# Four mixture-of-experts layers: the next pass's routing woven into the last combine of the pass before, and the first destination mask kept in program order

## The chip, the cores and the metric

The kernel runs on one core of a Trainium2 chip. That core has five engines, each with its own queue of instructions: TensorE (PE, matrix products; its weight loads are shown as PEld), VectorE (DVE), ScalarE (ACT), GpSimd (POOL) and SyncE (SP), which here only issues transfers. Engines wait for one another through semaphores. The metric is the device time of one execution in microseconds (us), the median of several runs.

## What is computed

The input `x` holds T = 2048 tokens of D = 256 numbers. Four layers follow each other; each adds half of a feed-forward block, then an attention block, then half of the same feed-forward block again, each on the layer-normed `x`:

```python
x = x + 0.5 * ffn(layernorm(x))
x = x + attn(layernorm(x))
x = x + 0.5 * ffn(layernorm(x))
```

So the feed-forward block of layer n runs twice, and the second run of layer n is followed at once by the first run of layer n + 1. The feed-forward block is a mixture of experts (layer 1; the others differ in sizes and details):

```python
logits = xf @ gate_w.T
probs = softmax(logits)
topk_p, topk_i = top_k(probs, 2)
h = silu(xf @ w1[e]) * (xf @ w2[e])      # for each expert e
y = sum over the token's two experts of topk_p * (h @ w3[e])
sh = silu(xf @ sw1.T) * (xf @ sw2.T) @ sw3.T   # the shared expert, every token
return y + sh
```

Layer 0 (f0) has 7 experts of width 128, weights by a sigmoid, and a limit on how many tokens an expert keeps. Layers 1 and 3 (f1, f3) have 8 experts of width 176; in f3 the shared expert is 704 wide and gated by a sigmoid for each token. Layer 2 (f2) has 16 experts of width 128 and a Gelu without a product. All numbers are fp32.

## The kernel before

**Blocks and passes.** The tokens are held on chip as 16 tiles of 128 rows, in NB = 4 blocks of 512 tokens (four tiles each). One run of a feed-forward block is one `Sparse` object, a pass. The text calls them 0a, 0b, 1a, 1b, 2a, 2b, 3a, 3b: layer, and first or second run. The object of the b pass is `now`, that of the next layer's a pass is `following`.

**Steps of a pass**, in the order of the program (`body`):

- `norm(j)` normalizes block j: on VectorE statistics (L290, L291), the variance (L269) and a reciprocal (L271) around a square root on ScalarE (L270), then four row tiles on ScalarE (L297). Each row tile also carries the token's number.
- `columns(j)` turns the rows with eight PE transposes (L280), copies them to `hT` on VectorE and ScalarE (L281), multiplies by the router (L788), copies (L796), turns back (L798) and copies the logits to `lg` (L800).
- `choose(j)` finds the best two experts of each token in a chain of small VectorE operations (L836 to L848).
- `place(j)` counts with two PE products how many tokens go to each expert before each token (L883, L884), works out the slot of each token on VectorE (L888 to L903), and lets POOL scatter the rows to their slots in memory (`sent`): eight indirect transfers a block (L913). Then `weigh(j)` makes the softmax weights of the block: two subtractions, two Exp on ScalarE (L865, L867), a sum, a reciprocal and two products.
- `tables()` works out on VectorE which expert each tile of 128 slots belongs to and where its rows lie (`r_which`, `r_row`). SP reads `r_row` before it fetches.
- The routed experts go tile by tile in a pipeline (`experts`): `fetch` loads four tiles of rows into `got` by SP (L1007) and makes on VectorE a mask and the destination rows (`d_m`, `d_has`, `d_dest`, L1011 to L1017, five small operations); `turn` transposes (L1027) and copies to `hs` (L1029); `first`, `flip` and `second` are the expert's products (L1042, L1060, L1072); POOL scatters the result back (L913).
- `combine(j)` loads the two results of each token (`mine`, by SP) and adds them to `x` with their weights: eight VectorE operations a block (L1099).

**The shared expert** (`glu_pieces`) is cut into pieces that `beside(amount)` puts between the other steps: for each chunk PE makes the products (`up`, L330), ScalarE the activation (L337; L334 in f2), VectorE the product `mid` (L338; none in f2); then four times PE multiplies by the second matrix (`y`, L345) and VectorE adds into `x` (L349). `ahead` says how many blocks of it may run before the routed experts (3 in f1, otherwise 2); `beside(1000)` puts what remains of them behind `tables()`; the other blocks come with the combines.

**What sets the order.** PE's order is the program's (a manual schedule). VectorE's order is the program's only around the combines, so for `combine` and what follows each of them; elsewhere a scheduler orders it, and an instruction marked with `keep_in_program_order` keeps its place. Whatever the order, an engine works through its queue in that order: an instruction whose input is missing holds up all behind it.

**At the end of a b pass** the loop over blocks is

```python
for j in range(NB):
    beside(7 if j else 10)
    while j >= self.ahead and self.shares <= j:
        beside(1)
    self.combine(j)
    after(j)
```

with `after` the next pass's `norm`. The next pass's `body(every, ...)` then arranges all four blocks: columns, choose, place. In a b pass blocks 0 and 1 are arranged inside the attention, and only blocks 2 and 3 in `body`.

Of the kernel before, what the change touches and what calls it, by code (L numbers as in the profile page):

```python
# [183 lines left out]
class Net:  # L184
# [80 lines left out]

    def rstd(self, out, var, scale, eps):

        nc = self.nc
        nc.vector.tensor_scalar(out, var, scale, eps, ALU.mult, ALU.add)  # L269
        nc.scalar.activation(out, out, AF.Sqrt)  # L270
        nc.vector.reciprocal(out, out)  # L271

# [11 lines left out]
    def norm_block(self, j, tiles):  # L284

        nc = self.nc
        mv = self.small.tile([P, 4, 2], F32, tag="mv", name="mv")
        for q in range(4):
            st = self.small.tile([P, 6], F32, tag="st", name="st")
            nc.vector.bn_stats(st, self.x[4 * j + q])  # L290
            nc.vector.bn_aggr(mv[:, q, :], st)  # L291
        rs = self.small.tile([P, 4], F32, tag="rs", name="rs")
        self.rstd(rs, mv[:, :, 1], 1.0, 1e-5)
        mr = self.small.tile([P, 4], F32, tag="mr", name="mr")
        nc.vector.scalar_tensor_tensor(mr, mv[:, :, 0], -1.0, rs, ALU.mult, ALU.mult)
        for q in range(4):
            nc.scalar.activation(  # L297
                tiles[q], self.x[4 * j + q], AF.Identity, bias=mr[:, q : q + 1], scale=rs[:, q : q + 1]
            )
# [18 lines left out]

    def glu_pieces(self, pool, hT, j, up, dn, func, scale, gate=None):


        nc = self.nc
        nch, nm = up.shape[1], up.shape[2]
        mids = []
        for c in range(nch):
            ps = []
            for m in range(nm):
                t = self.bank("up", 4)
                for k in range(KD2):
                    nc.tensor.matmul(t, lhsT=up[:, c, m, k, :], rhs=hT[:, k, :], start=(k == 0), stop=(k == KD2 - 1))  # L330
                ps.append(t)
            mid = pool.tile([P, 512], F32, tag="mid", name="mid", bufs=nch + 4)
            if nm == 1:
                nc.scalar.activation(mid, ps[0], func)  # L334
            else:
                act = pool.tile([P, 512], F32, tag="act", name="act", bufs=3)
                nc.scalar.activation(act, ps[0], func)  # L337
                nc.vector.tensor_tensor(mid, act, ps[1], ALU.mult)  # L338
            mids.append(mid)
            yield KD2 * nm  # L340
        for q in range(4):
            i = 4 * j + q
            y = self.bank("y")
            for c in range(nch):
                nc.tensor.matmul(  # L345
                    y[:, :D], lhsT=mids[c][:, q * P : (q + 1) * P], rhs=dn[:, c, :], start=(c == 0), stop=(c == nch - 1)
                )
            by = scale if gate is None else gate[:, i : i + 1]
            nc.vector.scalar_tensor_tensor(self.x[i], y[:, :D], by, self.x[i], ALU.mult, ALU.add)  # L349
            yield nch / 2  # L350

# [379 lines left out]
class Sparse:  # L731
# [7 lines left out]

    def __init__(self, net, w, n, e, width, func, gated=False, ahead=1, capacity=False, fill=None):  # L740


        self.net, self.nc, self.tc = net, net.nc, net.tc
        self.w, self.n, self.e, self.width, self.func = w, n, e, width, func
        self.gated, self.ahead, self.fill = gated, ahead, fill
        self.const = {k: net.c[k] for k in ("ones", "below", "ids", "later4")}
# [11 lines left out]
        self.normed = set()  # L758
        self.got, self.dest, self.hs, self.mids, self.midT, self.reg = {}, {}, {}, {}, {}, {}


# [8 lines left out]
    def norm(self, j):  # L770
        if j in self.normed:
            return
        self.normed.add(j)
        self.net.norm_block(j, self.net.row_tiles(j))
        ins = self.nc.vector.tensor_scalar(
# [4 lines left out]
    def columns(self, j):  # L780
        nc, net, e = self.nc, self.net, self.e
        hT = self.hT[j] = net.hT[j] = net.to_columns(net.row_tiles(j), j)
# [3 lines left out]
        for k in range(KD2):  # L786
            for q in range(4):
# [5 lines left out]
                    stop=(k == KD2 - 1),  # L793
                )
        rows = net.routes.tile([P, P], F32, tag="r_lgT", name="r_lgT", bufs=2)
        nc.vector.tensor_copy(rows, ps[:, :P])  # L796
        ps = net.bank("t")
        nc.tensor.transpose(ps[:, :P], rows, net.c["ident"])  # L798
        lg = self.lg[:, 4 * j : 4 * j + 4, :]
        nc.vector.tensor_copy(lg, ps[:, :P].rearrange("p (q e) -> p q e", e=32)[:, :, : self.lg.shape[2]])  # L800
# [52 lines left out]

    def weigh(self, j):

        nc, e = self.nc, self.e
        if self.capacity:
            nc.vector.tensor_scalar(
                self.wt[:, :, 4 * j : 4 * j + 4], self.wt[:, :, 4 * j : 4 * j + 4], 0.5, None, ALU.mult
            )  # L860
            return
        first, second = self.wt[:, 0, 4 * j : 4 * j + 4], self.wt[:, 1, 4 * j : 4 * j + 4]
        p = self.small([P, 4, e], "r_p")
        nc.vector.tensor_tensor(p, self.lg[:, 4 * j : 4 * j + 4, :e], first.unsqueeze(2).to_broadcast([P, 4, e]), ALU.subtract)
        nc.scalar.activation(p, p, AF.Exp)  # L865
        nc.vector.tensor_tensor(second, second, first, ALU.subtract)
        nc.scalar.activation(second, second, AF.Exp)  # L867
        m = self.small([P, 4], "r_m")
        nc.vector.tensor_reduce(m, p, AX.X, ALU.add)
# [4 lines left out]
    def place(self, j):  # L874
# [30 lines left out]
        for q in range(4):  # L905
            for k in range(2):
                self.scatter("to", self.net.sent, slot[:, k, q : q + 1], self.rows[:, 4 * j + q, :])
        self.weigh(j)

# [89 lines left out]
    def fetch(self, s):  # L999
# [10 lines left out]
        m = self.tile([P, self.G], "d_m", bufs=3)[:, :q]  # L1010
        nc.vector.tensor_tensor(m, t[:, :q, D + 1], self.less[:, s : s + q], ALU.not_equal)  # L1011
        nc.vector.scalar_tensor_tensor(m, m, float(T), number, ALU.mult, ALU.add)
# [90 lines left out]
    def arrange(self, blocks, beside):  # L1103

        for j in blocks[:2]:
            self.norm(j)
        if len(blocks) < NB:
            beside(7)
# [7 lines left out]

    def body(self, blocks, after):


        nc, net, n, e, cap = self.nc, self.net, self.n, self.e, self.capacity  # L1120
        with (
# [9 lines left out]
            self.edn = net.load(keep, f"{n}_edn", parts=2)  # L1131
            gate = None
            if self.gated:
                gate = keep.tile([P, NT], F32, tag="sgate", name="sgate")

            def shared(js):
                for j in js:
                    if self.gated:
                        by = slice(4 * j, 4 * j + 4)
                        nc.scalar.activation(gate[:, by], self.lg[:, by, e], AF.Sigmoid)  # L1140
                        nc.vector.tensor_scalar(gate[:, by], gate[:, by], 0.5, None, ALU.mult)
                    yield from net.glu_pieces(
                        mids, self.hT[j], j, self.w[f"{n}_up"], self.w[f"{n}_dn"], self.func, 0.5, gate
                    )
                    self.shares = j + 1

            self.shares = 0

            def other():
                if self.fill:  # L1150
                    for _ in range(22):
                        self.fill.step()
                        yield 1
                yield from shared(range(self.ahead))

            work = other()

            def beside(amount):
                while amount > 0:
# [3 lines left out]
                    amount -= done  # L1163

            with net.tc.manual_schedule(engines={mybir.EngineType.PE}):
                self.arrange(blocks, beside)
                if self.number == 1:
                    self.pad()
                self.tables()
                beside(1000)  # L1170
                if cap:
# [3 lines left out]
                if self.fill:  # L1175
                    self.fill.rest()
                work = shared(range(self.ahead, NB))
                if cap:
                    nc.vector.tensor_tensor(self.wt, self.wt, cap.kept, ALU.mult)
                with net.tc.manual_schedule(engines={mybir.EngineType.DVE}):  # L1180
                    for j in range(NB):
                        beside(7 if j else 10)
                        while j >= self.ahead and self.shares <= j:
                            beside(1)
                        self.combine(j)
                        after(j)

# [634 lines left out]
def kernel(ctx: ExitStack, tc: tile.TileContext, io, out: bass.AP):  # L1822
# [3 lines left out]

    def experts(n, w, fill=None):
        if n == 0:
            return Sparse(net, w, "f0", 7, P, AF.Silu, ahead=2, capacity=True, fill=fill)
        if n == 2:  # L1830
            return Sparse(net, w, "f2", 16, P, AF.Gelu, ahead=2)
        return Sparse(net, w, f"f{n}", 8, 176, AF.Silu, gated=(n == 3), ahead=(3 if n == 1 else 2))

# [23 lines left out]
    for n in range(4):  # L1857
        if n:
            w = layers[n].w
            with stage() as net.psum:  # L1860
                following.body(every, normed)
            now = experts(n, w)
            with stage() as net.psum:
                left = (attn1, attn2, attn3)[n - 1](net, w, now)
        if n < 3:
            layers[n + 1] = Layer(net, n + 1).load()
            following = experts(n + 1, layers[n + 1].w)
        with stage() as net.psum:
            now.body(left, following.norm if n < 3 else store)
        layers[n].stack.close()  # L1870
# [18 lines left out]
```

## Time and profile before

| | us |
|---|---|
| median of 3 runs (3324.53 to 3328.82) | 3327.32 |
| the profiled execution | 3326.3 |
| its span, from the first to the last instruction | 3324.5 |

| engine | busy us | share of the span |
|---|---|---|
| PE | 2972.3 | 89% |
| PEld (beside PE) | 2040.4 | 61% |
| DVE | 1764.3 | 53% |
| POOL | 1342.6 | 40% |
| ACT | 1260.2 | 38% |

The mean clock that the throttle granted PE is 0.936 of full speed. In the trace a pass begins some us before the one ahead of it has ended. The times from the span's start that the text needs: combine(0) of 0b at 1350.5 and the first turn of 1a at 1446.2 (transition 0b-1a); combine(0) of 1b at 2012.0 and the first turn of 2a at 2092.4 (1b-2a); combine(0) of 2b at 2691 and the first turn of 3a at 2796.6 (2b-3a). The first turn of 1b is at 1902.0, that of 3b at 3157.3. A "turn" is L1027.

How to read it: busy time is a sum over the span. What a change is worth is read from the stage it touches: from who waited last there. Some views show single instructions with the idle time of their engine before them and, behind an arrow, the instruction whose end released them.

### The profile page before, as it was taken

What the parts mean: (1) busy time and instruction counts of PE and PEld (TensorE: products, weight loads), DVE (VectorE), ACT (ScalarE), POOL (GpSimd) and SP (SyncE); (2) the same over time, 40 slices, a digit from 0 to 9 for tenths busy, and PEclk for the clock granted to TensorE, in tenths of its full rate; (3) what the DMA queues carried; (4) which work ended last, traced back from release to release, by engine and by line L of the source; (5) the groups of instructions that cost most, each with busy time, mean ns of one, the idle gap of its engine ahead of it and who ended that gap; (6) DMA issues with size and microseconds to landing.
All of it is one profiled execution on the core that took longest, in us unless ns stands there. A gap on an engine that the chain in (4) does not pass through costs nothing. (4 is left out here: it accounts for less than half of the span.)

```text
span 3324.5 us, 44449 instructions
## 1 busy us (share of the span) xinstructions
PE 2972.3 (89%) x14098; PEld 2040.4 (61%) x14098; DVE 1764.3 (53%) x4824; ACT 1260.2 (38%) x2755; POOL 1342.6 (40%) x1616
## 2 busy tenths in 40 slices
PE   5769999999999967798899896789998779988899
PEld 3647777777777746466455574644554546655575
DVE  4646666666666676634743336345775453344433
ACT  3333222333223333433623244434775452335331
POOL 3436666766667534333211133531334433302230
PEclk9889999999999988899999998887998889997999
DMA  6333333323211023433000324441112542312132
GB/s 214 120 101 91 93 97 98 102 83 89 86 43 42 29 100 118 149 100 128 9 13 26 114 90 151 153 117 45 32 33 78 175 161 89 99 35 68 58 92 90
DMA packets 203340, 300.01 MB, mean 90 GB/s; under 512 B 30200, under 2 KB 156792, under 8 KB 201752
## 3 DMA queue, kind: packets, MB, share of 16 engines
q1 hardware_dynamic: 174840, 219.67, 22.6%
q0 software_dynamic: 28272, 77.51, 6.6%
q8 instruction: 118, 1.93, 0.2%
q14 instruction: 110, 0.90, 0.1%
HBM read 178.78 MB, written 118.04 MB: 89 GB/s over the span
## 5 line engine op out<-in xcount | busy, mean ns | idle before, releaser
L913 POOL DMA_INDIRECT back<-res,d_dest x326 | 312.6, 959 | 532.6 <-ACT res L1076 436.2
L913 POOL DMA_INDIRECT sent<-rows,r_slot x256 | 247.8, 968 | 505.6 <-issue 371.7
L1042 PE MATMUL up<-f_eup,hs 128*128 x1304 | 356.4, 397 | 9.9 <-issue 8.6
L330 PE MATMUL up<-hT,f_up 128*128 128x512 f32 x704 | 327.2, 620 | 6.2 <-DVE mid L338 4.6
L1072 PE MATMUL y<-f_edn,midT 88*128 (+1 forms) x964 | 263.9, 383 | 0.0
L345 PE MATMUL y<-f_dn,mid 128*128 128x256 f32 x768 | 201.3, 416 | 52.3 <-DVE x L349 25.4
L1042 PEld LDWEIGHTS up<-f_eup,hs 128*128 128x128 f32 x1304 | 214.1, 196 | 54.2 <-issue 14.8
L330 PEld LDWEIGHTS up<-hT,f_up 128*128 128x128 f32 x704 | 140.2, 201 | 169.9 <-issue 158.0
L1029 DVE COPY hs<-t 128x256 f32<-128x256 f32 x326 | 137.6, 423 | 184.1 <-PE t L1027 183.8
L665 PE MATMUL up<-vo,hT 128*128 128x256 f32 x1024 | 226.7, 379 | 0.0
L545 ACT COPY mid<-up 128x256 f32<-128x256 f32 x192 | 71.4, 372 | 393.0 <-PE up L541 390.0
L546 DVE TENSOR_TENSOR o<-up,mid 128x512 f32<-128x512 f32 x192 | 132.5, 691 | 163.4 <-ACT mid L545 163.2
L665 PEld LDWEIGHTS up<-vo,hT 128*128 128x128 f32 x1024 | 194.3, 190 | 40.0 <-issue 15.0
L525 POOL TENSOR_TENSOR ddq<-d0q,d2q 128x256 f32<-128x256 f32 x128 | 218.4, 1737 | 0.0
L345 PEld LDWEIGHTS y<-f_dn,mid 128*128 128x128 f32 x768 | 155.1, 208 | 102.3 <-DVE mid L338 33.0
L1027 PE MATMUL t<-c_ident,got 128*128 128x128 f32 x652 | 132.8, 287 | 77.2 <-DMA got<-sent 65.5
L338 DVE TENSOR_TENSOR mid<-act,up 128x512 f32<-128x512 f32 x112 | 76.5, 686 | 215.4 <-PE up L330 191.2
L1048 ACT ACTIVATE eact<-up 128x176 f32<-128x176 f32 (+1 forms) x232 | 70.6, 304 | 313.6 <-PE up L1042 300.7
L1435 POOL TENSOR_SCALAR_AFFINE_SELECT p<-p 128x512 f32<-128x512 f32 (+1 forms) x192 | 92.4, 482 | 230.6 <-ACT p L1418 146.3
L1072 PEld LDWEIGHTS y<-f_edn,midT 88*128 88x128 f32 (+1 forms) x964 | 158.8, 192 | 15.6 <-ACT midT L1062 1.3
L1378 DVE TENSOR_REDUCE mx<-a 128x2 f32<-128x512 f32 (+1 forms) x192 | 123.9, 688 | 79.9 <-PE a L1377 79.6
L337 ACT ACTIVATE act<-up 128x512 f32<-128x512 f32 x112 | 66.7, 596 | 241.6 <-PE up L330 240.7
(358 smaller groups left out, 6374.6 us busy)
## 6 DMA issues: line engine op xcount, KB each, us to landing
got<-sent SPq DMA_DIRECT2D x326, 129.0 KB
sent<-rows SPq DMA_DIRECT2D x64, 516.0 KB
mine<-back SPq DMA_DIRECT2D x64, 512.0 KB
dbc<-dd SPq DMA_DIRECT2D x64, 384.0 KB
f_eup<-in_f_eup_dram SPq DMA_DIRECT2D x16, 704.0 KB
f_eup<-in_f_eup_dram SPq DMA_DIRECT2D x14, 512.0 KB
f_edn<-in_f_edn_dram SPq DMA_DIRECT2D x8, 704.0 KB
back<-res,d_dest POOLq DMA_INDIRECT x326, 2.4
```

The source lines that it names most:

```text
L330: nc.tensor.matmul(t, lhsT=up[:, c, m, k, :], rhs=hT[:, k, :], start=(k == 0), stop=(k == KD2 - 1))
L345: nc.tensor.matmul(y[:, :D], lhsT=mids[c][:, q * P : (q + 1) * P], rhs=dn[:, c, :], start=(c == 0), stop=(c == nch - 1))
L525: nc.gpsimd.tensor_tensor(dd[:, 2 * f, u], shifted(d0[:, f])[u], d2[:, f], ALU.subtract)
L546: nc.vector.tensor_tensor(o[:, i], sides.rearrange("p (u n) -> p u n", u=2), t.unsqueeze(1).to_broadcast([P, 2, N]), ALU.add,)
L665: nc.tensor.matmul(ps[:, u * 256 : (u + 1) * 256], lhsT=hT[j][:, k, q * P : (q + 1) * P], rhs=vo.vo[:, h, k, :], start=(k == 0), stop=(k = ...
L913: ins = self.nc.gpsimd.indirect_dma_start(out=out, out_offset=bass.IndirectOffsetOnAxis(ap=index, axis=0), in_=in_, in_offset=None).ins
L1027: nc.tensor.transpose(ps[:, k * P : (k + 1) * P], got[:, k * P : (k + 1) * P], self.net.c["ident"])
L1029: nc.vector.tensor_copy(t, ps[:, : KD2 * P].rearrange("p (k t) -> p k t", k=KD2))
L1042: nc.tensor.matmul(ps[:, :ncol], lhsT=hs[:, k, :], rhs=up[:, bass.ds(x, 1), k, :], start=(k == 0), stop=(k == KD2 - 1))
L1072: nc.tensor.matmul(y[:, :D], lhsT=midT[:, c, :], rhs=dn[:, bass.ds(x, 1), c, :], start=(c == 0), stop=(c == parts - 1))
L1378: nc.vector.tensor_reduce(out, by, AX.X, ALU.min, negate=True)
L1435: self.nc.gpsimd.affine_select(out=e, in_=e, pattern=[[0, n], [1, P]], compare_op=ALU.is_ge, fill=0.0, base=0, channel_multiplier=-1)
```

## The change

- `glu_pieces` is split: `glu_steps` yields, for each piece, `products` (PE and ScalarE) and `rest` (VectorE) as two calls, so that VectorE's part can be issued later than PE's.
- `norm` is split into `moments` (statistics, variance, square root) and `norm_rows` (the rest). `columns` is split into `columns_only` (to the router's product), `turn_logits` and `logits`.
- `weigh` runs once in a pass, for all 16 tiles, after `tables()`, and not once for each block at the end of `place`.
- The first `d_m` of each pass keeps its place in the program, so on VectorE it stands behind the pieces of the shared expert.
- The end of a b pass is `onward(then, issue, settle)`: between `combine(j)` and `norm(j)` of the pass stand columns, choose and place of the next pass's block j - 1, all in VectorE's written order, with pieces of the next pass's shared expert (`issue` calls products, `settle` the VectorE parts issued before). `early` says how many blocks of it may be used so (2 in f1 and f2, 1 in f3).
- So the next pass's `body` gets no blocks to arrange: it begins with `tables()`. The first run of f2 has `ahead` 3 in place of 2. The shared expert's buffers grow with `bufs`.

In the counts per engine VectorE has 114 instructions fewer, ScalarE 61 fewer (25 of them loads of an activation table); PE, POOL and SP issue as many as before. The core of the diff:

```diff
+    def glu_steps(self, pool, hT, j, up, dn, func, scale, gate=None, bufs=None):
         nc = self.nc
         nch, nm = up.shape[1], up.shape[2]
-        mids = []
-        for c in range(nch):
+        mids, acts, sums = {}, {}, {}
+        def chunk(c):
             ps = []
             for m in range(nm):
                 t = self.bank("up", 4)
                 for k in range(KD2):
                     nc.tensor.matmul(t, lhsT=up[:, c, m, k, :], rhs=hT[:, k, :], start=(k == 0), stop=(k == KD2 - 1))
                 ps.append(t)
-            mid = pool.tile([P, 512], F32, tag="mid", name="mid", bufs=nch + 4)
+            mids[c] = pool.tile([P, 512], F32, tag="mid", name="mid", bufs=bufs or nch + 4)
             if nm == 1:
-                nc.scalar.activation(mid, ps[0], func)
+                nc.scalar.activation(mids[c], ps[0], func)
             else:
                 act = pool.tile([P, 512], F32, tag="act", name="act", bufs=3)
                 nc.scalar.activation(act, ps[0], func)
-                nc.vector.tensor_tensor(mid, act, ps[1], ALU.mult)
-            mids.append(mid)
-            yield KD2 * nm
-        for q in range(4):
-            i = 4 * j + q
-            y = self.bank("y")
+                acts[c] = act, ps[1]
+        def gated(c):
+            if nm == 2:
+                act, ps = acts.pop(c)
+                nc.vector.tensor_tensor(mids[c], act, ps, ALU.mult)
+        def down(q):
+            y = sums[q] = self.bank("y")
             for c in range(nch):
                 nc.tensor.matmul(
                     y[:, :D], lhsT=mids[c][:, q * P : (q + 1) * P], rhs=dn[:, c, :], start=(c == 0), stop=(c == nch - 1)
                 )
+        def into(q):
+            i = 4 * j + q
             by = scale if gate is None else gate[:, i : i + 1]
-            nc.vector.scalar_tensor_tensor(self.x[i], y[:, :D], by, self.x[i], ALU.mult, ALU.add)
-            yield nch / 2
+            nc.vector.scalar_tensor_tensor(self.x[i], sums.pop(q)[:, :D], by, self.x[i], ALU.mult, ALU.add)
+        for c in range(nch):
+            yield KD2 * nm, lambda c=c: chunk(c), lambda c=c: gated(c)
+        for q in range(4):
+            yield nch / 2, lambda q=q: down(q), lambda q=q: into(q)
...
-    def weigh(self, j):
+    def weigh(self):
         nc, e = self.nc, self.e
         if self.capacity:
-            nc.vector.tensor_scalar(
-                self.wt[:, :, 4 * j : 4 * j + 4], self.wt[:, :, 4 * j : 4 * j + 4], 0.5, None, ALU.mult
-            )
+            nc.vector.tensor_scalar(self.wt, self.wt, 0.5, None, ALU.mult)
             return
-        first, second = self.wt[:, 0, 4 * j : 4 * j + 4], self.wt[:, 1, 4 * j : 4 * j + 4]
-        p = self.small([P, 4, e], "r_p")
-        nc.vector.tensor_tensor(p, self.lg[:, 4 * j : 4 * j + 4, :e], first.unsqueeze(2).to_broadcast([P, 4, e]), ALU.subtract)
+        full = [P, NT, e]
+        first, second = self.wt[:, 0], self.wt[:, 1]
+        p = self.tile(full, "r_p", bufs=1)
+        nc.vector.tensor_tensor(p, self.lg[:, :, :e], first.unsqueeze(2).to_broadcast(full), ALU.subtract)
         nc.scalar.activation(p, p, AF.Exp)
         nc.vector.tensor_tensor(second, second, first, ALU.subtract)
         nc.scalar.activation(second, second, AF.Exp)
-        m = self.small([P, 4], "r_m")
+        m = self.tile([P, NT], "r_sum", bufs=1)
         nc.vector.tensor_reduce(m, p, AX.X, ALU.add)
         nc.vector.reciprocal(first, m)
         nc.vector.tensor_scalar(first, first, 0.5, None, ALU.mult)
...
-        self.weigh(j)
...
-        nc.vector.tensor_tensor(m, t[:, :q, D + 1], self.less[:, s : s + q], ALU.not_equal)
+        ins = nc.vector.tensor_tensor(m, t[:, :q, D + 1], self.less[:, s : s + q], ALU.not_equal)
+        if s == 0:
+            self.tc.keep_in_program_order(ins)
...
+    def onward(self, then, issue, settle):
+        for j in range(NB + 1):
+            p = j - 1
+            if j < NB:
+                if j:
+                    self.beside(7)
+                while j >= self.ahead and self.shares <= j:
+                    self.beside(1)
+                self.combine(j)
+            settle()
+            if p >= 0:
+                ps = then.columns_only(p)
+            if j < NB:
+                of = self.net.moments(j)
+            if p >= 0:
+                ps = then.turn_logits(ps)
+            if j < NB:
+                then.norm_rows(j, *of)
+            if p >= 0:
+                issue()
+                then.logits(p, ps)
+                then.choose(p)
+                then.place(p)
+                settle()
+                issue()
+    def body(self, blocks, after=None, then=None):
...
                 self.tables()
+                self.weigh()
                 beside(1000)
...
-                work = shared(range(self.ahead, NB))
+                work = self.shared(mids, range(self.ahead, NB), bufs)
                 if cap:
                     nc.vector.tensor_tensor(self.wt, self.wt, cap.kept, ALU.mult)
                 with net.tc.manual_schedule(engines={mybir.EngineType.DVE}):
-                    for j in range(NB):
-                        beside(7 if j else 10)
-                        while j >= self.ahead and self.shares <= j:
-                            beside(1)
-                        self.combine(j)
-                        after(j)
+                    if then:
+                        beside(10)
+                        nch = then.w[f"{then.n}_up"].shape[1]
+                        steps = enumerate(then.shared_steps(mids, range(then.early), bufs))
+                        late = []
+                        def settle():
+                            while late:
+                                late.pop(0)()
+                        def issue():
+                            for i, (_, products, rest) in steps:
+                                i %= nch + 4
+                                if i == nch:
+                                    settle()
+                                products()
+                                late.append(rest)
+                                if i < nch or (i - nch) % 2:
+                                    return True
+                        self.onward(then, issue, settle)
+                    else:
+                        for j in range(NB):
+                            beside(7 if j else 10)
+                            while j >= self.ahead and self.shares <= j:
+                                beside(1)
+                            self.combine(j)
+                            after(j)
+                if then:
+                    while issue():
+                        settle()
+                    settle()
...
-            return Sparse(net, w, "f2", 16, P, AF.Gelu, ahead=2)
-        return Sparse(net, w, f"f{n}", 8, 176, AF.Silu, gated=(n == 3), ahead=(3 if n == 1 else 2))
+            return Sparse(net, w, "f2", 16, P, AF.Gelu, ahead=3 if first else 2, early=2)
+        return Sparse(
+            net, w, f"f{n}", 8, 176, AF.Silu, gated=(n == 3), ahead=(3 if n == 1 else 2), early=(2 if n == 1 else 1)
+        )
 
...
-                following.body(every, normed)
+                following.body([], normed)
...
-            following = experts(n + 1, layers[n + 1].w)
+            following = experts(n + 1, layers[n + 1].w, first=True)
         with stage() as net.psum:
-            now.body(left, following.norm if n < 3 else store)
+            if n < 3:
+                now.body(left, then=following)
+            else:
+                now.body(left, store)
         layers[n].stack.close()
```

## The prediction

> **What bounds the kernel now.** I read the page first: PE is busy 89% of the span, so the time changes only where PE stands still or runs at half clock, at a stage whose end the next one needs. So I went to what PE waited for over the whole run (total us, times, longest us):
>
> ```profile
> PE t L1027 <- DMA got<-sent: 65.5, 5, 20.4
> PE y L345 <- DVE x L349: 25.4, 7, 5.4
> PE y L345 <- DVE mid L338: 23.2, 12, 7.1
> PE up L330 <- DVE mid L338: 4.6, 2, 4.0
> ```
>
> The first row is the start of the routed experts (L1027 turns the first gathered rows). The next three are the shared expert: PE waits for VectorE to multiply `mid` or to add into `x`. The longest of them, 7.1 and 4.0, are single events in the passes 1b and 3b. VectorE's timeline at the first (start, us, engine, what; in brackets the idle time before it and its releaser), then at the second:
>
> ```profile
> 1867.76 0.69 DVE L338 TENSOR_TENSOR mid<-act,up 128x512 f32<-128x512 f32 x1 [2.56 <-PE up L330]
> 1875.48 0.16 DVE L1011 TENSOR_TENSOR d_m<-got,r_less 128x4 f32<-128x4 f32 x1 [7.03 <-DMA got<-sent]
> ...
> 1878.32 0.69 DVE L338 TENSOR_TENSOR mid<-act,up 128x512 f32<-128x512 f32 x1
> ```
>
> ```profile
> 3129.05 0.16 DVE L1011 TENSOR_TENSOR d_m<-got,r_less 128x4 f32<-128x4 f32 x1 [8.90 <-DMA got<-sent]
> ...
> 3131.48 0.69 DVE L338 TENSOR_TENSOR mid<-act,up 128x512 f32<-128x512 f32 x1
> ```
>
> VectorE stands in order at `d_m`, whose gather has not landed, and a ready `mid` is queued behind it. PE then pays again at half clock. Stretches (length; busy PE, PEld, DVE, ACT, POOL; granted clock; DMA share; GB/s), the stalls of 1b and 3b first, then the transitions 0b-1a, 1b-2a, 2b-3a:
>
> ```profile
> 1871.00:1879.00 8.00, 0.95 (x5) 0.49 (x3) 1.91 (x10) 0.00 (x0) 0.00 (x0) 0.72 0.70 187
> 1879.00:1886.00 7.00, 6.94 (x19) 5.68 (x20) 2.10 (x11) 0.00 (x0) 0.00 (x0) 0.59 0.05 15
> 1886.00:1893.00 7.00, 7.00 (x18) 3.23 (x18) 1.15 (x3) 1.19 (x2) 0.00 (x0) 1.00 0.00 0
> ...
> 3132.00:3138.00 6.00, 5.77 (x8) 2.50 (x9) 2.85 (x12) 0.00 (x0) 0.00 (x0) 0.55 0.10 28
> ```
>
> ```profile
> 1364.00:1446.00 82.00, 63.76 (x252) 36.57 (x253) 45.73 (x219) 32.14 (x48) 30.69 (x32) 0.86 0.43 136
> ...
> 2030.00:2103.00 73.00, 37.78 (x176) 24.72 (x177) 44.97 (x209) 28.79 (x50) 32.99 (x33) 0.69 0.30 97
> ...
> 2720.00:2797.00 77.00, 67.44 (x263) 40.45 (x263) 36.88 (x166) 30.72 (x44) 30.91 (x32) 0.91 0.32 95
> ```
>
> Three transitions, three limits. In the first PE is idle 18 of 82 us, waiting for VectorE's chain. In the second PE has 38 us of work in 73, and the end is POOL's: 32 scatters of rows (L913) run from 2046.5 to 2088.6, one each 1.27 us. In the third PE is busy from 2745 to the first turn at 2796.6, though the gather landed at 2778.
>
> **The change, part by part.** Durations are this execution's. Its time is 3326.3 us (span 3324.5); the median of the runs is 3327.3, so I add 1.0 at the end.
>
> *The first d_m in program order.* It now stands behind the last add into `x` of the shared pieces, so what queues behind a late gather is only the first `hs` copies, which need the gather too. 1b: the 7.1 goes; what is late next is that `mid` itself, with its activation (0.60) and product (0.69), of which two y matmuls (0.4) cover some: 0.9 stays. Half clock at 0.59 over 7 us lost 2.9 us of full-clock work; a short wait may keep some, I take 2.5. After the stall PE is busy to the first turn at 1902, long after the gather, so all of it reaches the end: -8.7 (bounds -6.2, -9.1). 3b: 4.0 less 0.5, and 6 us at 0.55 lost 2.7, of which 2.5: -6.0 (-3.5 to -6.7). Against it, two or more groups of five small VectorE operations (0.2 apart) now come beside the first turns: +0.3 in each of five passes, +1.5 (0 to +4).
>
> *Transition 0b-1a.* Before, the four choices (router columns, choose, place) follow the four combines and share VectorE with Exp waits; place's matmuls come at 1376.4, 1393.4, 1404.8, 1416.2. After, combine(1) still follows the adds of block 3 (ends 1362.9), and one block's period on VectorE, in order, is: combine 8 x 0.396 = 3.17; `mid` 0.69; `hT` copy 0.69; statistics 4 x 0.53 = 2.1; variance to Sqrt's end, with its table load (1.283), 1.73; reciprocal and two small ones 0.4; logits 0.2; choose, 12 steps of 0.22, 2.5; place's matmuls and back 0.97; place 1.5; a second `mid` 0.69. Sum 14.8. Place(0) on PE: 1362.9 + 0.7 + 2.1 + 0.2 + 1.7 + 0.4 + 0.2 + 2.5 = 1370.7; two periods, then a last of some 10 without combine and norm: 1410. After it PE has the y of block 1 (6.2), block 2 (10.5 and 6.2) and perhaps one chunk (3.6), 26.5, so the first turn is at 1437 instead of 1446.2, about when the gather can land. The pieces between a block's logits and its place take 3.6 at full clock, under the chain's 4.8, but up to 7.2 at half clock: 2.4 more in each period puts it at 1442. Ends: -9 and, with place(3) 5 us late, +2. The former `d_m` stalls here (3.1 and 2.0) are in these. I take -5: PE has 11.7 us of work in 14.8 and should mostly keep its clock.
>
> *Transition 1b-2a.* Combine(1) waits as before for the late adds of block 3 (2024.6). Place(0): 2024.6 + 3.2 + 0.7 + 2.1 + 0.2 + 1.7 + 0.4 + 0.3 + 3.0 (64 columns, 0.25 a step) = 2036; scatters start at 2039.5, 7 earlier. But blocks then come each 14.2 and not each 10.9: 2053.7, with two adds 2068.8, and eight scatters take 10.1, so the last block's start at 2079 and end at 2089. POOL's gain at the front is lost to its gaps: 0 (-2 to +8). The tables, with the weights now ahead of them, are ready about 2088, just in time. A third block's shared expert moves into PE's idle 2072 to 2092. That shortens the end of 2a: there the add of block 3 between combine(0) and (1) held VectorE from 2180.03 to 2183.58 and PE had both left blocks; with one block I take -3.4 (0 to -7). Fewer half-clock us at the experts' start: -1 (0 to -2).
>
> *Transition 2b-3a.* Place(3) at about 2759 both ways; PE is the bound with the same 24 up and 24 y matmuls: 0 (-5 to +6). On SP's queue three loads of the next experts' weights stand ahead of the last `mine`, as they do in 1b-2a now; the gather of `mine` is early there: 0.
>
> *Weights once per pass.* 114 VectorE and 61 ScalarE instructions go, 25 of these table loads of 1.283. In the passes inside a layer PE's fill covers them (no wait of PE names Exp): -1 (0 to -3). SP's and POOL's instruction counts do not change.
>
> Sum: -8.7 - 6.0 + 1.5 - 5 + 0 - 3.4 - 1 + 0 - 1 = -23.6, from 3326.3 to 3302.7; with 1.0, 3303.7, say 3303.5.
>
> [...]
>
> **The rivals.** (1) *Slower: the interleaved loop runs at half clock.* PE's gaps in each block (waits for `hT`, `r_lgT`, `r_both`, up to 3.8 in the trace) keep the clock at 0.50, as it was from 2042 to 2050. Then both pieces of a block (3.6) take up to 7.2 and come ahead of place and of the next columns: period 14.8 + 2.4 + 3.6 = 20.8. 0b-1a: 1370.7 + 41.6 + 16 + 26.5 = 1454.8, +9. 1b-2a: place(3) 2094, scatters to 2106, +18. 2b-3a: +12. With the other terms (-18.6) the sum is +20: 3347. It decides from a period of about 19. Against it: 0.86 and 0.91 granted in two of the three.
> (2) *About the same: the stalls only move.* Period 17 to 18: 0b-1a 0, 1b-2a +8, 2b-3a +5, `d_m` and the rest -18: -5, 3322. For it: three of the loop's waits are PE's and VectorE's for one another, each of which shows 1 to 3 us now.
> (3) *More: 2b-3a gains as well* (5), 0b-1a reaches its -9, 2a's end -7, 1b and 3b their full 15.8: 3288. Against it: PE is busy from 2745.
>
> **How the numbers follow.** Likeliest 0.56; slower 0.15; the same 0.15; more 0.14. The range 3286 to 3326 leaves out the slower rival (0.15) and a little below the largest gain; the likeliest alone is 3292 to 3316, by the bounds of the transitions. This kernel tells 0.2% (6.7 us) from no change, so faster is below 3320.7: the likeliest, the largest gain and a third of the second rival, 0.75; within 0.10; slower 0.15.
>
> **What would show it.** PE's waits for `mid` (L338) of 7.1 and 4.0 are gone, `d_m` comes after the last add in 1b and 3b, and first turns there are 8.7 and 6 earlier relative to the pass's start. Place's matmuls come 14 to 15 apart in 0b-1a. In 1b-2a POOL has gaps of 4 between its eights of scatters and the gather starts about when it did. It is wrong if these periods exceed 17, if the granted clock there falls below 0.7, or if the last tables come later than the last scatter.

## The result, and the profile after

The changed kernel takes 3295.25 us (median of six runs, 3289.1 to 3301.11), the kernel before in the same runs 3325.93 (3319.27 to 3332.25): a ratio of 0.9909, 95% interval 0.9897 to 0.9921, so 26 to 34 us less. The forecast was 3303.5. The profiled execution took 3293.35 us (span 3291.6).

What PE waited for over the whole run (total us, times, longest us), the rows that answer to those of before:

```profile
PE t L1077 <- DMA got<-sent: 50.2, 4, 17.4
PE y L369 <- DVE x L376: 30.3, 10, 5.4
...
PE y L369 <- DVE mid L364: 13.5, 10, 3.3
```

The long waits for `mid` are gone: 23.2 became 13.5, none is over 3.3, and the separate row of 4.6 for `up` has dropped out. PE waits more for the adds into `x`: 30.3 in ten waits, after 25.4 in seven. VectorE's timeline in 1b shows why (start, us, engine, what; in brackets the idle time ahead and its releaser):

```profile
1867.34 0.69 DVE L364 TENSOR_TENSOR mid<-act,up 128x512 f32<-128x512 f32 x1 [2.75 <-PE up L351]
...
1888.44 0.42 DVE L376 SCALAR_TENSOR_TENSOR x<-y,x 128x256 f32<-128x256 f32 x1 [0.87 <-PE y L369]
1888.78 0.22 DVE L1059 TENSOR_TENSOR d_m<-got,r_less 128x4 f32<-128x4 f32 x2
```

`mid` waits only for PE's own products, and `d_m` (now L1059) comes after the last add of the shared expert, with no idle time. PE keeps its clock there. First two stretches of 1b, where 0.72 and 0.59 were granted before, then the three transitions from combine(0) to the first turn (columns as before; the clock is the number ahead of the last two):

```profile
1860.00:1868.00 8.00, 8.00 (x21) 3.61 (x19) 2.04 (x3) 1.80 (x4) 4.05 (x5) 1.00 0.23 83
1868.00:1875.00 7.00, 7.00 (x27) 5.05 (x27) 1.73 (x5) 0.58 (x1) 0.00 (x0) 1.00 0.63 165
...
1353.00:1442.00 89.00, 67.06 (x271) 40.23 (x272) 58.36 (x224) 28.92 (x44) 31.78 (x32) 0.87 0.49 146
1997.00:2077.00 80.00, 49.24 (x211) 30.92 (x210) 57.88 (x215) 21.99 (x37) 32.42 (x32) 0.78 0.40 145
2668.00:2772.00 104.00, 84.55 (x330) 50.89 (x329) 58.36 (x223) 40.33 (x59) 31.81 (x32) 0.90 0.41 132
```

The prediction's stretches of before begin later in the transitions. From combine(0) to the first turn the profile of before has:

```profile
1350.50:1446.20 95.70, 68.88 (x269) 40.31 (x270) 57.35 (x255) 35.01 (x54) 30.69 (x32) 0.84 0.43 135
2012.00:2092.40 80.40, 38.42 (x185) 24.50 (x184) 53.11 (x228) 29.40 (x47) 32.03 (x32) 0.73 0.39 142
2691.00:2796.60 105.60, 85.74 (x328) 50.43 (x327) 60.02 (x256) 46.07 (x69) 30.91 (x32) 0.89 0.41 130
```

To see where the time went I cut both traces at the same events: the first turn of each pass, and its first and last combine. The stages that differ by more than a us, and 1b-2a (us; the columns behind "change" are experiments told below, "no loop" with both its profiles):

| stage | before | change | again | mask only | loop, no mask | weights | third block | no loop |
|---|---|---|---|---|---|---|---|---|
| 0b-1a: combine(0) to first turn | 95.6 | 88.4 | 88.3 | 88.1 | 91.9 | 94.2 | 96.6 | 85.0, 86.6 |
| last combine of 1a to first turn of 1b | 312.6 | 302.9 | 302.9 | 302.3 | 312.9 | 312.0 | 312.4 | 302.8, 303.0 |
| 1b-2a: combine(0) to first turn | 80.4 | 79.6 | 79.3 | 79.7 | 79.5 | 81.0 | 79.5 | 81.6, 80.8 |
| combines of 2a | 25.3 | 21.8 | 21.8 | 26.2 | 21.8 | 26.1 | 21.8 | 21.8, 21.8 |
| last combine of 2a to first turn of 2b | 409.5 | 405.3 | 408.0 | 405.6 | 408.9 | 405.4 | 409.0 | 407.1, 407.7 |
| 2b-3a: combine(0) to first turn | 105.8 | 104.2 | 105.8 | 104.1 | 104.9 | 105.5 | 105.5 | 102.3, 101.7 |
| combines of 3a | 59.3 | 57.6 | 60.6 | 59.0 | 57.6 | 57.6 | 59.3 | 60.4, 57.6 |
| last combine of 3a to first turn of 3b | 191.6 | 183.6 | 185.1 | 186.9 | 185.7 | 184.9 | 191.5 | 184.3, 186.3 |

Between before and change these rows give -36.7; the stages not shown give +3.9 back (2.7 of it in the attention of layer 0, which is 1031.6 to 1036.1 long in the runs of all these kernels and not by any edit). Together that is the difference of the spans, 32.8.

### The profile page after: what moved, and what is told of

It is laid out like the page before. It is cut to its first block, busy times and chain, and to the rows that moved or that the text cites. A ratio compares the mean times of both kernels' runs of the same rounds, so it can differ in the third digit from the quotient of the medians.

```text
span 3291.6 us, 44235 instructions
## 1 busy us (share of the span) xinstructions
PE 2953.8 (90%) x14069; PEld 2035.0 (62%) x14098; DVE 1766.9 (54%) x4710; ACT 1222.3 (37%) x2694; POOL 1348.2 (41%) x1616
## 5 line engine op out<-in xcount | busy, mean ns | idle before, releaser
L1092 PEld LDWEIGHTS up<-f_eup,hs 128*128 128x128 f32 x1304 | 213.3, 195 | 54.9 <-issue 15.4
L369 PE MATMUL y<-f_dn,mid 128*128 128x256 f32 x768 | 194.7, 406 | 46.4 <-DVE x L376 30.3
```

What stands on the lines that cost most here:

```text
L369: nc.tensor.matmul(y[:, :D], lhsT=mids[c][:, q * P : (q + 1) * P], rhs=dn[:, c, :], start=(c == 0), stop=(c == nch - 1))
L1092: nc.tensor.matmul(ps[:, :ncol], lhsT=hs[:, k, :], rhs=up[:, bass.ds(x, 1), k, :], start=(k == 0), stop=(k == KD2 - 1))
```

## The experiments

The theory behind the forecast was that the mask's place on VectorE gives most (14.7 of 23.6), the third block of shared work at 2a 3.4, and the woven loop some 5 at 0b-1a. Its rival was that the loop is what counts. I did each part alone, and undid each.

**The mask alone.** On the kernel before:

```diff
-        nc.vector.tensor_tensor(m, t[:, :q, D + 1], self.less[:, s : s + q], ALU.not_equal)
+        ins = nc.vector.tensor_tensor(m, t[:, :q, D + 1], self.less[:, s : s + q], ALU.not_equal)
+        if s == 0:
+            self.tc.keep_in_program_order(ins)
```

> The kernel before with one edit: the first d_m of each pass keeps its place in the program. Theory A (most of the gain is this mask's place on VectorE): the stalls of 1b (7.1 us and its half clock) and 3b (4.0 and its half clock) go, -9.5 and -7, and in 0b-1a the stalls of 3.1 and 2.0 with the half clock behind them, -5 to -8: 19 to 24 us less than before, some 3303. Theory B (the woven loop brings most): only the bare waits count, since another wait for the gather takes their place: 5 to 10 less, 3317 to 3321.

Measured: 3299.06, ratio 0.9927 (0.9911 to 0.9943), 24 us less. Of its trace, PE's waits for `mid`:

```profile
PE y L345 <- DVE mid L338: 11.0, 9, 3.3
```

The place of one mask in each pass gives four fifths of the gain (24 of 30 by the ratios; the intervals of the two kernels overlap): 10.3 in 1b, 7.6 in 0b-1a, 4.7 in 3b. The first theory holds; the new fact is 0b-1a, where the mask alone already gives all of the 7.2 that the whole change gives. There before had these waits for `mid` between combine(0) and the first turn, and this clock behind them:

```profile
PE y L345 <- DVE mid L338: 6.4, 4, 3.1
...
1437.00:1441.00 4.00, 2.02 (x6) 1.51 (x5) 1.92 (x8) 0.00 (x0) 0.00 (x0) 0.57 0.48 133
1441.00:1446.00 5.00, 5.00 (x17) 4.08 (x16) 1.40 (x6) 0.00 (x0) 0.00 (x0) 0.66 0.00 0
```

With the mask alone:

```profile
PE y L345 <- DVE mid L338: 1.3, 2, 0.8
...
1435.00:1441.00 6.00, 6.00 (x27) 4.65 (x26) 1.96 (x4) 0.00 (x0) 0.00 (x0) 1.00 0.79 220
```

**The loop without the mask.** The changed kernel with those lines taken out again.

> The changed kernel without that edit: the scheduler is free with the first d_m again. Theory A: 1b and 3b get their stalls back (+16.5); 0b-1a keeps part of its gain: 3312, 12 to 15 us under before. Theory B: 3300 to 3304, the loop keeps the gain. If the scheduler now puts d_m elsewhere by itself, PE's waits for mid in 1b and 3b say so.

Measured: 3314.06, ratio 0.9963 (0.9949 to 0.9977). In 1b the old picture is back (VectorE's timeline of this kernel):

```profile
1864.48 0.69 DVE L364 TENSOR_TENSOR mid<-act,up 128x512 f32<-128x512 f32 x1 [2.56 <-PE up L351]
1872.26 0.16 DVE L1059 TENSOR_TENSOR d_m<-got,r_less 128x4 f32<-128x4 f32 x1 [7.09 <-DMA got<-sent]
...
1875.01 0.69 DVE L364 TENSOR_TENSOR mid<-act,up 128x512 f32<-128x512 f32 x1
```

1b loses its 9.7. 3b doesn't lose all of its 8.0: it keeps 5.9, without the mask. The next run says why. 0b-1a keeps 3.7 of its 7.2; the weights alone (next run) give 1.4 there, so without the mask's edit the loop may gain some 2 of its own, no more than such rows differ by.

**The weights alone.** On the kernel before, `weigh` as in the change, once behind `tables()`:

```diff
-        self.weigh(j)
...
                 self.tables()
+                self.weigh()
```

> The kernel before with the weights made once in a pass. Theory A: PE's fill covers the Exp and their table loads, 0 to -3 us (3323 to 3326). Theory B: the unexplained 4 us at 2b, and part of 3b, come from fewer table loads ahead of place: -6 to -10.

Measured: 3318.32, ratio 0.9975 (0.9964 to 0.9986): 8 us less, not 1. In 3b the last scatter of rows starts 153.6 after the last combine of 3a and not 155.5, so the gather lands earlier against PE's work and the stall is shorter. VectorE's timeline and PE's wait in 3b of this kernel:

```profile
3102.94 0.68 DVE L338 TENSOR_TENSOR mid<-act,up 128x512 f32<-128x512 f32 x1
3121.94 0.16 DVE L1009 TENSOR_TENSOR d_m<-got,r_less 128x4 f32<-128x4 f32 x1 [8.18 <-DMA got<-sent]
3122.81 0.69 DVE L338 TENSOR_TENSOR mid<-act,up 128x512 f32<-128x512 f32 x1
```

```profile
PE up L330 <- DVE mid L338: 1.7, 1, 1.7
```

4.0 of waiting became 1.7, and the clock no longer fell behind it. The last 60 us ahead of the first turn of 3b, first in before, then in this kernel:

```profile
3097.20:3157.20 60.00, 54.11 (x194) 33.32 (x193) 21.30 (x83) 11.75 (x18) 15.50 (x16) 0.94 0.20 62
...
3086.00:3146.00 60.00, 56.75 (x206) 34.73 (x205) 23.92 (x92) 12.67 (x19) 15.46 (x16) 1.00 0.20 62
```

So in 3b mask and weights take away the same stall: 4.7 and 6.7 alone, 8.0 and 6.5 together in the two profiles of the change. The time is in the second theory's range, its 4 us at 2b are a separate matter (below).

**The third block alone.** On the kernel before:

```diff
-            return Sparse(net, w, "f2", 16, P, AF.Gelu, ahead=2)
+            return Sparse(net, w, "f2", 16, P, AF.Gelu, ahead=3 if first else 2)
```

> The kernel before with a third block of the shared expert ahead of the routed experts in 2a (ahead 3 for the first run of f2). Theory A: it fills PE's idle at the start of 2a and shortens the end of 2a by 3.4, with a shorter half clock 1 more: -3 to -5, 3321 to 3323. Theory B: the end of 2a is set by the loads of mine and VectorE's combines: 0 to -1.

Measured: 3321.35, ratio 0.9985 (0.9976 to 0.9994), 5 us less. The combines of 2a take 21.8 and not 25.3 in every kernel with this edit, and in none without. Settled.

**The change again**, beside the next three runs.

> The changed kernel as it is, beside the next three. 3295 again; its profile says which of the differences between stages come again. [...]

Measured: 3300.85, ratio 0.9917 (0.9898 to 0.9937). The stage of attention ahead of 2b takes 408.0 here and took 405.3 in the first profile of the same kernel, and 404.0 to 409.5 in the other kernels, in no order of their edits. The 4 us from 409.5 before to 405.3 are not shown to be the change's; a row of the table says something only beyond some 3 us, unless it comes again.

**No loop.** The three small edits together on the kernel before, with the combines and the routing as they were.

> The kernel before with the mask's place, the weights once and the third block ahead in 2a, all without the woven loop: its transitions are as before. Theory A (the loop gains nothing of its own): 3291 to 3297, the changed kernel's time or a little less; the first turn of 1a comes 88 us after combine(0) of 0b, as with the mask alone. Theory B (the loop is worth the 5 us given for 0b-1a and more): 3300 to 3305.

Measured: 3286.81, ratio 0.9876 (0.9855 to 0.9898). Once more, on another chip:

> The kernel without the loop once more, for the interval: 3285 to 3292, transitions of 85, 81.6 and 102.

Measured: 3287.61, ratio 0.9876 (0.9861 to 0.9891). This is below even the first theory's range, and 0.3 to 0.4% less than the change, whose interval touches this one's only at the end. The loop isn't worth its place. Start of place's products (L884, L933 in the change) and the first turn of 1a, us after combine(0) of 0b, with the experiments that follow; the distance from one place to the next is called the period:

| kernel | place 0, 1, 2, 3 | first turn | left after the last place |
|---|---|---|---|
| before | 26.1, 43.0, 54.5, 65.8 | 95.6 | 29.8 |
| mask alone | 25.2, 43.4, 54.8, 66.1 | 88.1 | 22.0 |
| change | 20.9, 36.9, 51.6, 62.0 | 88.4 | 26.4 |
| no loop | 26.3, 40.6, 52.0, 63.0 | 85.0 | 22.0 |
| no loop, second profile | 25.1, 40.5, 53.6, 64.6 | 86.6 | 22.0 |
| change, third piece | 22.6, 39.0, 54.0, 67.6 | 84.5 | 16.9 |
| change, weights in the loop | 21.3, 38.1, 54.0, 66.1 | 93.2 | 27.1 |
| change, no pieces | 19.5, 32.1, 44.6, 54.0 | 103.3 | 49.3 |

The loop brings the first place some 5 earlier, then loses most of it again with periods of 16.0 and 14.7, against 14.3 and 11.4, or 15.4 and 13.1, without it. VectorE's waits show what differs: in the one written chain it stands still until place's products and the square root come back. First the change, 63 us from combine(0) on, then the same stretch without the loop, where a scheduler chose the order of the routing. There no wait for the square root is in the list, and the longest is for `up` (9.4 in five, against 3.1 in the change):

```profile
DVE r_add L937 <- PE t L933: 5.4, 3, 2.4
DVE rs L306 <- ACT rs L270: 3.1, 3, 1.4
```

```profile
DVE r_add L887 <- PE t L883: 0.8, 1, 0.8
```

And 4.4 more are left after the last place: PE's timeline shows five chunks of `up` ahead of it in the loop and six in the old arrangement, a chunk being 3.6. The transitions of the change add up to 272.2 and 273.4, those without the loop to 268.9 and 269.1. That is 3 to 4.5 us; the medians differ by 8 to 14. The rest is not shown in any stage: both profiled executions without the loop (3294.46, 3293.14) were the slowest of their runs, and in them the attention of layer 0, which no edit touches, took 1036.1 and 1033.5, where before has 1031.7.

**A third piece in each turn of the loop.**

```diff
                 of = self.net.moments(j)
             if p >= 0:
+                issue()
                 ps = then.turn_logits(ps)
...
-                                if i == nch:
+                                if i >= nch and (i - nch) % 2 == 0:
                                     settle()
...
+ early 3 in f1 and f2, 2 in f3
```

> The changed kernel with a third piece of the next shared expert in each turn of the loop, put on PE between the router's product and the turn of the logits, where PE waits for VectorE. A pair of y pieces now has its adds made before the next pair is issued. Theory A (PE's work after the loop sets 0b-1a and 2b-3a, and the gaps are free): each of the four turns takes a chunk of 3.6 out of what is left after the loop and lengthens the period by 1 to 2: -4 to -8 in 0b-1a and in 2b-3a, 0 to +3 in 1b-2a; 3284 to 3292. Theory B (the loop is paced by PE at half clock): the period grows by the whole chunk and the transitions stay or lose 2 to 4 each: 3295 to 3305.

Measured: 3301.45, ratio 0.992 (0.9902 to 0.9937), the same as the change. That is the second theory's time, though 0b-1a is 84.5 (-3.9), near what the first theory had. But 1b-2a grows to 83.7, since the last place there comes 5.6 later (66.1 for 60.5) and POOL's scatters with it, and 2b-3a stays at 104.0: its last place comes at 74.9 and not at 63.7. One transition gains, one pays, and the third stays.

**The weights in the loop again.** The changed kernel with the old `weigh(j)` at the end of `place`.

> The changed kernel with the weights made block by block at the end of place again, so with two Exp and their table loads inside the written VectorE order of the loop. Theory A: VectorE waits in each of twelve turns for one or two loads of 1.28 and the Exp, 2 to 4 us a turn: periods of 17 to 19 and not 15, of which 0b-1a passes on 3 to 8, 1b-2a 6 to 10, 2b-3a 0 to 4: 3306 to 3316. [...] Theory B: ScalarE's loads lie beside VectorE's other work: 3295 to 3300.

Measured: 3320.73, ratio 0.9984 (0.9973 to 0.9996): 20 us or more lost to the change, over the first theory's range. The periods are not over what it gave (17 to 19): the first two are 17.4 and 17.8 and not 14.8 in 1b-2a, and 15.9 to 17.2 in the other transitions. The transitions are 93.2, 90.4 and 115.0, together 25 or 26 longer than in the change; 2b-3a, with 9 to 11 for 0 to 4, is what the theory had most too low. ScalarE in 1b-2a (busy us, mean ns; idle ahead), and VectorE's new wait there:

```profile
L915 ACT ACT_TABLE_LOAD x3 | 3.8, 1283 | 0.1
...
L915 ACT ACTIVATE r_p<-r_p 128x64 f32<-128x64 f32 x4 | 1.0, 256 | 12.5 <-DVE wt L916 9.3 <-DVE r_p L914 3.2
```

```profile
DVE r_m L919 <- ACT r_p L915: 6.0, 4, 3.6
```

A wait of 1.5 on average for load and Exp, and six small operations of 0.2, make up the 2.6 to 3.0 in each period of 1b-2a. So within the loop the change needs its own edit to the weights; outside it, that edit gives 8.

**The loop at 1b-2a only**, where POOL's scatters and not PE's left-over work end last (75.6 after combine(0) in the change, with the first turn at 79.6).

```diff
-                following.body([], normed)
+                following.body([] if n == 2 else every, normed)
...
-            if n < 3:
+            if n == 1:
                 now.body(left, then=following)
             else:
-                now.body(left, store)
+                now.body(left, following.norm if n < 3 else store)
```

> The changed kernel with the woven loop at 1b-2a alone; the other two transitions arrange their blocks as before. Theory A (the loop costs 3 to 4 us where PE's shared expert is left over after it, 0b-1a and 2b-3a, and gains 2 where POOL's scatters end last, 1b-2a): transitions of 85, 79.5 and 102, and 2 less than without any loop, 3284 to 3291. Theory B (the differences between the loops are how the clock fell): transitions of 88, 80 and 104 like the changed kernel, 3295 to 3301.

Measured: 3290.02, ratio 0.9884 (0.987 to 0.9898). The transitions are 86.6, 79.5 and 99.1, the first theory's side; but the whole is not faster than without any loop. A gain of 2 there can't be told. 2b-3a, arranged here as without the loop, is 2.6 to 3.2 shorter than there, but the stretch ahead of it, from the first turn of 2b to combine(0), is 5 to 6 longer.

**The loop without pieces.** `early` 0 in all passes.

> The changed kernel with no piece of the next shared expert in the loop (early 0); all of them come after the tables. Theory A (VectorE's chain of waits sets the period): the period falls only by the two products, from 15 to 13.4 or 14, the last place comes 5 earlier, and the 50 us (1a) and 63 us (3a) of shared work are left to do: 0b-1a 105 to 108, 2b-3a 118 to 123, 1b-2a 76 to 80; 3325 to 3340. Theory B (PE's pieces at half clock set the period): the period falls by 4 or more, to 11 or less, as without the loop.

Measured: 3334.96, ratio 1.0027 (1.0017 to 1.0037), 9 us over before. The periods fall to 12.6 and 12.5 in 0b-1a, 13.3 in 1b-2a and 13.7 in 2b-3a: by 1 to 3.4, not to 11, though PE has almost nothing to do and its clock falls:

```profile
1351.00:1454.00 103.00, 69.61 (x268) 42.05 (x269) 58.59 (x223) 19.93 (x37) 31.29 (x32) 0.75 0.44 124
2010.00:2095.00 85.00, 47.04 (x209) 30.43 (x209) 57.82 (x213) 18.24 (x34) 32.33 (x32) 0.70 0.44 150
2681.00:2803.00 122.00, 88.72 (x329) 53.88 (x328) 59.43 (x223) 31.43 (x52) 31.28 (x32) 0.79 0.35 114
```

So VectorE's chain, with its waits, sets most of the period (14.8 less two products of 0.69 is 13.4, 0.9 more than 0b-1a shows). 1b-2a took 85.2 where 76 to 80 were expected: POOL's last scatter ends 73.5 after combine(0), earlier than in the change (75.6), but PE has 24 `up` and 48 `y` left after the last place and is busy for 24.3 of the 25.7 us to the first turn. Without pieces in the loop that work ends last there, and not POOL's. The pieces are what lets the loop break even.

**More shared work ahead of place, without the loop**: `beside(8 if self.e == 8 else 5)` for `beside(5)`.

> The kernel without the loop, with more of the shared expert ahead of each place in the passes with 8 experts (beside 8 in place of 5: one more piece or two in each block). If PE's gaps there are free, the last place of 1a and 3a comes 0 to 4 later and 7 to 10 us less are left after it: 0-1a and 2b-3a 3 to 6 shorter each, 3278 to 3283. If the pieces push place back by their own length, the transitions stay: 3285 to 3292.

Measured: 3291.37, ratio 0.9896 (0.9879 to 0.9912). 0b-1a is 84.9 and 2b-3a 99.6, some 2 shorter each than in the second profile without the loop, but 0b-1a no shorter than in the first, and 2b-3a was 99.1 without this edit (the loop at 1b-2a only). The time is not below 3287. No gain is shown.

## Why the prediction was right, and where it was off

*The first d_m in program order: right.* 1b gained 9.7 where 8.7 was given (a little over the bounds, 6.2 to 9.1: both the bare wait of 7.1 and the whole half clock, 0.59 over 7 us, went), 3b 8.0 and 6.5 where 6.0 was given. The +1.5 for the mask's small operations beside the first turns doesn't show: the routed experts' own stretches changed by -0.8 to +2.1, within what repeats differ by.

*Transition 0b-1a: right in time, for the wrong part.* Place was worked out at 20.2, 35.0, 49.8 and 60 after combine(0) and came at 20.9, 36.9, 51.6 and 62.0; 26.5 was given as left, and 26.4 was. The periods of 16.0 and 14.7 are a little over the 14 to 15 that I named. The gain of 7.2 lies between my -5 and my -9. (The worse end, +2, doesn't come out of its own numbers: 1442 and 5 more is 1447, less than 1 late.) But the step compared the loop with before as it stood, stalls and all. Against the kernel with the mask's stalls gone (88.1) the loop gives nothing, against no loop with the weights made once (85.0, 86.6) it costs 2 to 3. The step that failed is "The former `d_m` stalls here (3.1 and 2.0) are in these": taking them away gives all of it, without the loop.

*Transition 1b-2a: right.* The first place comes 5 earlier, the last scatters end within 1 us of the same time: -0.8 for 0 and -1. *The end of 2a: right*, -3.5 for -3.4, shown by the third block alone. *Transition 2b-3a: right in time*, -1.6 and 0.0 for 0, but not by a place(3) that stays: it comes 4.4 earlier in the first profile and 2.8 in the second. After it PE has the same 48 `up` and 72 `y` matmuls left as before, and they take 40.5 and not 37.7, with a wait of 2.2 for an add into `x` among them. Without the loop the transition is 102.3 and 101.7, so here too the loop costs 2 or more.

*Weights once per pass: mis-sized.* I gave -1 (0 to -3), "PE's fill covers them". Alone the edit measures -8 (interval -5 to -12). The cover fails where the gather is what PE waits for in the end: in 3b the scatters start earlier (the last at 153.6 for 155.5), and the mask's stall with them is shorter (1.7 for 4.0). In 3b that is the stall which the mask takes away too, so there the two don't add. The parts alone (24, 8 and 5) give 37; all three without the loop give 40, the same within the intervals. The change gives 31 because the loop takes some of it back.

*The sum: near, in part by luck.* Without the -5 that I gave the loop at 0b-1a, my terms add up to -18.6. The three small edits without the loop measure -40, some 9 to 11 of it in 0b-1a by the profiles, where I had put the gain down to the loop. And the loop, which I gave -5, costs 8 to 14 by the medians. The small edits were set too low by more than half, the loop's cost was left out, and the two offset one another: -30.7 measured for -23.6.

*The rivals.* The slower one, a loop at half clock with a period of 20.8, didn't come: the granted clock in the transitions is 0.87, 0.78 and 0.90, against 0.84, 0.73 and 0.89 before, and the period 15 to 16. In 1b-2a PE did stand at 0.50 from 2028 to 2040, and the periods were 14.8 all the same. The "stalls only move" case didn't come either: no wait for `mid` over 3.3 is left. The result lies between the likeliest case and the larger gain; 1b, 3b and 0b-1a each gave 0.5 to 2.2 more than I had.

## What to carry to other kernels

When a change has many parts, compare each with the kernel in which the others are already made: here, in the forecast, the large part (a new order by hand) took credit for a stall that one line removed. Look first for a cheap instruction that waits for a transfer in the middle of an engine's queue; its price was more than the wait: in 1b 7.1 us of PE's time, and 0.59 of full clock granted over the 7 us behind it. Writing VectorE's order by hand brought the first block forward here (20.9 for 26.1), but gave up overlap of blocks that the scheduler had found (periods of 16.0 and 14.7, against 14.3 and 11.4, or 15.4 and 13.1), so it has to be judged by the last block and by what is left to do after it.

## What the runs showed of the hardware

A change of the activation table cost its load, and no more was seen: with two Exp a block back in the loop, the three loads of L915 are 1283 ns each with 0.1 us idle ahead of all three, and the periods of 1b-2a grew by 2.6 to 3.0, which the wait and the small operations make up. In the profile of before all 143 loads take 1283 ns, and 83 of them have less than 0.1 us of idle on either side.

A stall of PE did not always cost clock. Behind those of 7.1 and 4.0 us before (1b, 3b), 0.59 and 0.55 were granted, and 0.57 and then 0.66 behind 3.1 and 2.0 close together (0b-1a). Around single waits of 1.7 us (3b, weights alone) and 3.3 us (the combines of 3a, in the change) it stayed at 1.00; before, 0.74 was granted in the 6.6 us behind that same wait of 3.3. So a wait of PE that was made shorter gained more than the wait: in 3b 2.3 of waiting went and the stage became 6.7 shorter.

Executions of one and the same kernel differed by more than I had expected: 3289.1 to 3304.6 for the change, with whole stages of attention that no edit touches at 1034.4 or 1031.6, and at 405.3 or 408.0.
